# Absolute values of the inspected weights on VectorE instead of ScalarE, and the branch flag made just before the last block of P @ V

## The chip, the cores and the metric

The kernel runs on one core of one Trainium2 chip. The metric is device time of one execution in microseconds, the median of several runs. A separate execution is taken with the hardware profiler; its trace gives the rows shown here, with times counted from the start of its span.

The engines are named as in the profile: PE (TensorE, matmuls; PEld is its weight load), DVE (VectorE), ACT (ScalarE), POOL (GpSimd) and SP (SyncE, which issues most of the DMAs).

## The reference

The kernel computes one transformer layer on x of shape (2, 2048, 256), in float32:

```
xn = layernorm(x)
q, k, v = xn @ Wq, xn @ Wk, xn @ Wv                  # 256 wide, one head
P = softmax(causal(q @ k.T) / 16)
attention = (P @ v) @ Wo
h = silu((xn @ w1.T) * w1_s) * ((xn @ w2.T) * w2_s)  # 1024 wide
h = gelu((h @ h1.T) * h1_s)                          # h1, h2 are 1024 x 1024
h = gelu((h @ h2.T) * h2_s)
out = x + attention + (h @ w3.T) * w3_s
```

w1, w2, h1, h2 and w3 are drawn with entries -1, 0 and 1. The kernel does not rely on it: it looks at the weights as they are and branches.

## The kernel before, in words

**Two stages.** The attention stage runs to about 287 us of the span. Then every engine reads a one-word flag and branches: to the feed-forward part for ternary weights (taken here, `ffn_ternary`, to the end of the span) or to a general one (`ffn`).

**Attention.** The two sequences are cut into eight blocks of 512 rows, n = 0 to 7, four per sequence. Each block has four tiles t of 128 rows. Wk is folded into Wq and Wo into Wv beforehand. For each tile:

- `score` multiplies queries with keys into one of four PSUM banks that are used in turn (`bank()`, ps_0 to ps_3; L401, the causal mask in L407). VectorE copies the bank to SBUF and takes the row maximum on the way (L410). That copy is what frees the bank. After the last bank of a tile comes the negated maximum (L416), the exponential on ScalarE (L422) and, for the wider tiles, a transpose of 32 x 32 blocks on VectorE (L292). Its result is stored to DRAM (d) and fetched back rearranged (e, L304, four DMAs on SP), which completes the transpose of P.
- `turn` makes the two halves of the transposed P: the high half is a cast on ScalarE (L460), the low half a subtraction on GpSimd (L461). Narrow tiles are transposed by TensorE instead (L465), with the halves made by ScalarE (L251) and VectorE (L252).
- `weigh` multiplies both halves with the values, one block of 512 keys at a time (L479 with the high half, L484 with the low half). After the last block of a tile ScalarE scales by the inverse row sum (L499), and GpSimd adds two parts (L500).

Between these the projections of later blocks run: keys (L338, L339), queries (L357) and values (L373). They take their PSUM banks from the same four.

**Looking at the weights.** Beside the attention work, a list `looks` brings weights in by pieces of 128 x 1024 (fetched from the ScalarE queue, L622, into two tags of staging tiles, stg). For the h1 weights VectorE first forms four sums of quarters (L153), which are the factors of a fast matrix product, and SP stores them (L581). Then every piece of h1 and h2 goes through `odd`: take the absolute value in place (L565, ScalarE), then count the elements t for which (t != 0) != t (L567, VectorE), that is, those whose magnitude is neither 0 nor 1. There are sixteen such pieces. Pieces of w1, w2 and w3 go through `low` (L558, a bitwise AND on VectorE; L560, a sum on ScalarE). Each count is one column of `low_bits`.

When all pieces have been looked at, the largest column per partition is taken (L742), a matmul with a column of ones adds it over the partitions (L744), and a cast to an integer makes the flag (L745). In the program this stands at the end of the iteration in which the last look was placed. Each engine loads the flag into a register (L1175) and branches (L1176). Ahead of the branch TensorE has one more piece of work, the last quarter of the first feed-forward block (L172).

**What sets the order.** The program is written as one stream; a layer below reorders each engine's instructions by a model of their times when the program is built, so that moving one instruction can shift others on every engine. `tc.issue_after(mark)` keeps an instruction behind a marked one: marks["DVE"] is the latest score copy (L410), marks["ACT"] the latest exponential, marks["PE"] the latest L484 matmul. On the chip each engine works through its own list in order, a DMA issue included, and waits on semaphores.

Of the kernel before, what the change touches and what calls it, by code (L numbers as in the profile page):

```python
# [9 lines left out]
F32 = mybir.dt.float32  # L10
# [3 lines left out]
U32 = mybir.dt.uint32  # L14
AF = mybir.ActivationFunctionType
ALU = mybir.AluOpType
AX = mybir.AxisListType
# [3 lines left out]
P = 128  # L21
TB = 512
NT = TB // P
# [15 lines left out]
STEPS = [("A11", "B11"), ("S1", "T1"), ("S2", "T2"), ("S4", "B22"), ("S3", "T3"), ("A12", "B21"), ("A22", "T4")]  # L39

SLOTS = {"h1": range(7), "h2": (0, 4, 1, 3, 2, 5, 6)}
LOW_BITS = 0xFFF


# [20 lines left out]
def attn_ffn_kernel(  # L65
# [35 lines left out]
    nc = tc.nc  # L101
# [3 lines left out]
    N = B * NB  # L105
# [14 lines left out]
    flag = const.tile([1, 1], I32, name="flag")  # L120
# [68 lines left out]
    with ExitStack() as actx:  # L189
# [9 lines left out]
        small = actx.enter_context(tc.tile_pool(name="small", bufs=4))  # L199
# [6 lines left out]
        def in_turn(key, tiles):  # L206
            turns[key] += 1
            return tiles[(turns[key] - 1) % len(tiles)]

        def bank():  # L210
            return in_turn("ps", ps_tiles)
# [27 lines left out]
        ones = cp.tile([P, 1], F32, name="ones")  # L239
# [9 lines left out]
        def hi_lo(hi, lo, src):  # L249

            nc.scalar.copy(hi, src)  # L251
            nc.vector.tensor_tensor(lo, src, hi.bitcast(F32), ALU.subtract)  # L252
# [131 lines left out]
        marks = {}  # L384
# [49 lines left out]
        def by_blocks(n, t, m):  # L434
            kt = (n % NB) * NT + t + 1
            u = (m % NB) * NT // UK * UK
            return min(UK, kt - u) >= LEAST and (n, t) != (N - 1, NT - 1)
# [8 lines left out]
        def turn(n, t, m):  # L446
# [20 lines left out]
                )  # L467
            hi_lo(pT[:, 0, :w], pT[:, 1, :w], pt[:, :w])

        def weigh(n, t, m):  # L470
            first = n - n % NB
            st = state[n, t]
            if m == first:
                st["po"] = ps_o.tile([P, 2, D], F32, tag="po", name=f"po_{n}_{t}")
            tiles = NT if m < n else t + 1
            pT = st.pop(m)

            for j in range(tiles):
                nc.tensor.matmul(  # L479
                    out=st["po"], lhsT=pT[:, 0, ts(j, P)], rhs=vs[m][:, j, :, :],  # L480
                    start=(m == first and j == 0), stop=False,
                )
            for j in range(tiles):
                marks["PE"] = nc.tensor.matmul(  # L484
                    out=st["po"][:, 0, :], lhsT=pT[:, 1, ts(j, P)], rhs=vs[m][:, j, 0, :],
                    start=False, stop=(m == n and j == tiles - 1),
                ).ins
            if m == n:
                total = small.tile([P, 1], F32, tag="total", name=f"total_{n}_{t}")
                nc.vector.reduce_sum(total, st["sums"][:, : (n - first) * NT // UK + 1], axis=AX.X)  # L490
                inv = small.tile([P, 1], F32, tag="inv", name=f"inv_{n}_{t}")
                nc.vector.reciprocal(inv, total)
                if n not in attn:
                    attn[n] = rp.tile([P, NT + 1, D], F32, tag="r", name=f"r_{n}"), []
                r, made = attn[n]

                up = n < NB
                two = r[:, ds(t, 2), :]
                nc.scalar.activation(two, st["po"], AF.Copy, scale=inv)  # L499
                nc.gpsimd.tensor_tensor(two[:, int(up), :], two[:, 0, :], two[:, 1, :], ALU.add)  # L500
                made.append(t)
                if len(made) == NT:
                    assert made == sorted(made, reverse=up)
                    nc.sync.dma_start(out=r_d[n], in_=r[:, ds(int(up), NT), :].rearrange("p t d -> p (t d)"))
                del state[n, t]

        def score_steps(n, t):
            order = list(range(n - n % NB, n + 1))
            return [
                (6 * (TB if m < n else (t + 1) * P), lambda m=m: score(n, t, m, order))  # L510
                for m in order
            ]

        def weigh_steps(g, until):

            steps = []
            while g < len(blocks) and blocks[g][0] <= until:
                while turned[0] <= min(g + LEAD, len(blocks) - 1) and (
                    turned[0] <= g or blocks[turned[0]][0] <= until + 1
                ):  # L520
                    b = blocks[turned[0]]
                    steps.append((0 if by_blocks(*b[1:]) else 2 * TB, lambda b=b: turn(*b[1:])))
                    turned[0] += 1
                _, n, t, m = blocks[g]
                steps.append((6 * TB if m < n else 6 * P * (t + 1), lambda b=blocks[g]: weigh(*b[1:])))
                g += 1
            return g, steps
# [13 lines left out]
        low_bits = cp.tile([P, 32], F32, name="low_bits")  # L541
        looked = [0]
        looks = []

        def seen():
            looked[0] += 1
            return low_bits[:, looked[0] - 1 : looked[0]]
# [4 lines left out]
        def low(tiles, dst):  # L552
# [4 lines left out]
            with tc.issue_after(marks["DVE"]):  # L557
                nc.vector.tensor_scalar(tb, tb, LOW_BITS, None, ALU.bitwise_and)  # L558
            with tc.issue_after(marks["ACT"]):
                nc.scalar.activation(t, tb, AF.Copy, accum_out=seen())  # L560

        def odd(t):

            with tc.issue_after(marks["ACT"]):
                nc.scalar.activation(t, t, AF.Abs)  # L565
            with tc.issue_after(marks["DVE"]):
                nc.vector.scalar_tensor_tensor(  # L567
                    t, t, 0.0, t, ALU.not_equal, ALU.not_equal, accum_out=seen()
                )
# [21 lines left out]
        def item_signs(src):  # L591
            items.append(([src], [(0, lambda t: odd(t[0]))]))
# [26 lines left out]
        def fetched_weights(i):  # L619
            for src in items[i][0]:  # L620
                t = stgp.tile([P, SC], F32, tag="stg", name=f"stg_{i}_{len(tiles_of[i])}")
                nc.scalar.dma_start(out=t, in_=src)  # L622
                tiles_of[i].append(t)
# [4 lines left out]
        looks = [(0, lambda: fetched_weights(0))]  # L628
# [73 lines left out]
        def before(j):  # L702
            if 3 <= j < 3 + NB:
                n = NB + j - 3
                x1 = xs[n] = load_x(n)
                with tc.issue_after(marks["DVE"]):
                    stats(x1, mv1[:, j - 3], n)
            if j == 3 + NB:
                with tc.issue_after(marks["ACT"]):
                    r = root(mv1.rearrange("p n t k -> p (n t) k"), NB * NT, "1")  # L710
                for i in range(NB):
                    rstds[NB + i] = [a[:, ts(i, NT)] for a in r]
            if j in TURN_KEYS:
                turn_keys(NB + TURN_KEYS.index(j))
# [2 lines left out]
        now = 0  # L717
        until = -1
        j = -1
        checked = False  # L720
        while until < len(tiles) - 1:
            j += 1
            while until + 1 <= j - AHEAD:
                delay = DELAY_BLOCKS if by_blocks(*tiles[until + 1], 0) else DELAY
                if j <= len(tiles) and now < scored[until + 1] + delay:
                    break
                until += 1
            before(j)
            a = []
            if j < len(tiles):  # L730
                a = score_steps(*tiles[j])
                if j == 0:
                    a = []
            a = a + extra.get(j, [])
            weighed, b = weigh_steps(weighed, until)
            now += sum(cost for cost, _ in a + b)
            scored.append(now)
            merged(a, b, beside)
            if not looks and not checked:
                checked = True  # L740
                most = small.tile([P, 1], F32, tag="most", name="most")
                nc.vector.reduce_max(most, low_bits[:, : looked[0]], axis=AX.X)  # L742
                pf = bank()
                nc.tensor.matmul(out=pf[:1, :1], lhsT=most, rhs=ones, start=True, stop=True)  # L744
                nc.vector.tensor_copy(flag, pf[:1, :1])  # L745

        assert checked
        last_quarter = [bank(), bank()]
        with tc.issue_after(marks["PE"]):
            gated_products(last_quarter, xh0, HK - 1)  # L750
# [1 line left out]
    def ffn_ternary(actx):  # L752
# [208 lines left out]
        def fetch_factors():  # L961
            while factor_order and len(factor_tiles) < 3:
# [3 lines left out]
                    out=w.bitcast(F32).rearrange("p c o -> p (c o)"),  # L966
                    in_=factors[layer][:, SLOTS[layer][step]].rearrange("p c o -> p (c o)"),
                )
# [205 lines left out]

    some = nc.values_load(flag[0:1, 0:1], min_val=0, max_val=LOW_BITS * SC * P)  # L1175
    with tc.If(some == 0) as cmp:  # L1176
# [45 lines left out]
```

## Time and profile before

| | us |
|---|---|
| median of 3 runs (lowest to highest) | 871.73 (871.02 to 874.87) |
| the profiled execution's own time | 872.82 |
| its span | 871.1 |
| PE busy (share of the span) | 852.2 (98%) |
| DVE busy | 620.4 (71%) |
| ACT busy | 504.9 (58%) |
| POOL busy | 296.4 (34%) |
| mean granted TensorE clock | 0.990 |

The shares are averages over both stages. [...] In the rows, "x4" is the number of instructions merged into one row; the bracket at the end of a row gives the idle time of that engine just before it and what ended it.

### The profile page before, as it was taken

The numbers are of one execution on the slowest core, as the hardware profiler recorded it, in microseconds if no ns is written. First come the engines' busy times: TensorE is split into PE (matmuls) and PEld (weight loads), VectorE is DVE, ScalarE is ACT, GpSimd is POOL, SyncE is SP. The second block draws the span as 40 slices with busy tenths as digits, with TensorE's granted clock in tenths as the row PEclk, the third lists the DMA queues.
The fourth block names the chain that finished last, engine by engine and source line by source line (L and its number), as shares of the span: only waits on it lengthen the run. The fifth ranks groups of instructions, "written<-read, shape, count | busy, mean of one in ns | idle before, by whom it ended". The sixth has DMA issues, their size and how long they took to land.

```text
span 871.1 us, 12205 instructions
## 1 busy us (share of the span) xinstructions
PE 852.2 (98%) x4280; PEld 720.1 (83%) x4280; DVE 620.4 (71%) x1065; ACT 504.9 (58%) x881; POOL 296.4 (34%) x242
## 2 busy tenths in 40 slices
PE   8999799999999999999999999999999999999997
PEld 5988688888887878888988888988888898888887
DVE  5687664784764699996596596569468648848764
ACT  2556556764666456677256586536557635657670
POOL 4034857433544476550142050025024003502300
PEclk8999989999999999999999999999999999999999
DMA  9876499766792898854334434432444431144411
GB/s 307 331 250 212 152 348 292 265 214 194 251 343 62 340 400 309 312 192 146 111 109 150 144 144 146 148 121 103 146 145 145 146 136 58 50 144 145 145 49 53
DMA packets 62679, 162.53 MB, mean 187 GB/s; under 512 B 6544, under 2 KB 36368, under 8 KB 53264
## 3 DMA queue, kind: packets, MB, share of 16 engines
q1 hardware_dynamic: 56048, 141.73, 46.6%
q10 hardware_dynamic: 5472, 15.73, 5.3%
q0 software_dynamic: 1088, 4.19, 1.2%
q8 instruction: 36, 0.59, 0.3%
q14 instruction: 35, 0.29, 0.1%
HBM read 120.21 MB, written 47.71 MB: 193 GB/s over the span
## 4 chain that ended last, share of the span: by engine, by line
PE 75%; DMA 9%; DVE 6%; issue 3%; ACT 3%; POOL 2%; SPq 2%; ACTq 0%; POOLq 0%; DVEq 0%
PE ps_own L850 23%; PE ps L850 23%; PE ps L172 5%; PE ps_own L172 5%; PE ps L401 5%; DMA e<-d 4%; PE ps_own L1011 4%; PE ps L1011 4%; POOL pT L461 2%; DMA d<-b 2%; PE ps L373 2%; PE po L479 2%; PE ps L357 2%; SPq L304 1%; DMA d_x<-b 1%
## 5 line engine op out<-in xcount | busy, mean ns | idle before, releaser
L401 PE MATMUL ps<-k,q 128*128 128x512 f32 (+3 forms) x480 | 109.6, 366 | 0.0
L461 POOL TENSOR_TENSOR pT<-e,pT 128x512 fp32r<-128x512 f32 (+3 forms) x60 | 74.8, 1264 | 72.5 <-ACT pT L460 55.6
L401 PEld LDWEIGHTS ps<-k,q 128*128 128x128 f32 x480 | 82.0, 189 | 12.2
L479 PE MATMUL po<-v,pT 128*128 128x512 f32 x272 | 79.6, 406 | 6.6 <-ACT pT L460 6.5
L982 POOL TENSOR_TENSOR rt<-rt,xt 128x1024 f32<-128x1024 f32 x8 | 21.5, 2706 | 165.2 <-issue 114.7
L871 ACT ACTIVATE k_h_u<-k_h_u,h_s_sb 128x512 f32<-128x512 f32 x64 | 45.9, 722 | 38.1 <-DVE k_h_u L870 37.5
L830 POOL TENSOR_TENSOR k_h_u<-k_h_p,k_h_u 128x512 f32<-128x512 f32 x16 | 23.2, 1452 | 123.1 <-ACT q L185 106.3
L479 PEld LDWEIGHTS po<-v,pT 128*128 128x128 f32 x272 | 48.1, 193 | 14.5 <-ACT pT L460 7.2
L410 DVE TENSOR_SCALAR_CACHE_REDUCE s<-ps 128x512 f32<-128x512 f32 (+3 forms) x80 | 47.1, 600 | 12.1 <-PE ps L407 8.1
L422 ACT ACTIVATE s<-s,low 128x1024 f32<-128x1024 f32 (+7 forms) x48 | 43.0, 898 | 21.7 <-DVE low L416 21.7
L292 DVE STREAM_TRANSPOSE b<-s 128x1024 f32<-128x1024 f32 (+3 forms) x30 | 33.5, 1128 | 22.8 <-ACT s L422 20.5
L460 ACT CAST pT<-e 128x512 fp32r<-128x512 f32 (+3 forms) x60 | 32.4, 574 | 27.4 <-DMA e<-d 25.0
L484 PEld LDWEIGHTS po<-v,pT 128*128 128x128 f32 x272 | 42.0, 190 | 6.5 <-POOL pT L461 1.7
L484 PE MATMUL po<-v,pT 128*128 128x256 f32 x272 | 46.9, 286 | 0.2 <-POOL pT L461 0.2
L186 DVE TENSOR_TENSOR q<-k_h_u,q 128x512 fp32r<-128x512 f32 x32 | 45.9, 1462 | 0.0
L889 POOL TENSOR_TENSOR k_h_p<-f_h_B,k_h_p 128x512 f32<-128x512 f32 x16 | 34.4, 2175 | 21.2 <-DVE h_h_T L186 21.2
L500 POOL TENSOR_TENSOR r<-r 128x256 f32<-128x256 f32 x32 | 24.4, 765 | 49.7 <-ACT r L499 49.7
L830 POOL TENSOR_TENSOR f_w_B<-f_w_B,f_w_B 128x512 f32<-128x512 f32 x16 | 26.0, 1646 | 33.0 <-DVE f_w_B L181 33.0
L172 PE MATMUL ps<-xh,w_sb 128*128 128x512 f32 x144 | 35.9, 392 | 0.0
L870 DVE TENSOR_TENSOR k_h_u<-ps_own,k_h_u 128x512 f32<-128x512 f32 x32 | 21.7, 686 | 17.8 <-PE ps_own L850 17.8
L871 ACT ACTIVATE k_h_p<-k_h_p,h_s_sb 128x512 f32<-128x512 f32 x32 | 22.8, 722 | 18.6 <-DVE k_h_p L870 18.6
L850 PE MATMUL ps<-q,w_h_A 128*128 128x512 f32 x128 | 31.2, 393 | 1.5 <-DVE f_w_B L181 1.5
(176 smaller groups left out, 2201.3 us busy)
## 6 DMA issues: line engine op xcount, KB each, us to landing
w_h_S<-factors_h SPq DMA_DIRECT2D x32, 1024.0 KB, 4.7
w_h_A<-factors_h SPq DMA_DIRECT2D x24, 1024.0 KB, 4.7
d<-b SPq DMA_DIRECT2D x18, 512.0 KB, 3.5
e<-d SPq DMA_DIRECT2D x72, 128.0 KB, 3.6
xT_d<-k SPq DMA_DIRECT2D x8, 1024.0 KB, 7.3
stg<-in_ffn_h_w ACTq DMA_DIRECT2D x16, 512.0 KB, 5.6
x<-in_attn_x SPq DMA_DIRECT2D x16, 256.0 KB, 5.9
factors_h<-xh SPq DMA_DIRECT2D x4, 1024.0 KB, 4.8
```

The costliest lines, as they stand in the source:

```text
L172: nc.tensor.matmul(out=p, lhsT=w[:, c, ts(o, P)], rhs=xh[:, c, a, :], start=(c == 0 and a == 0), stop=(c == DC - 1 and a == 1),)
L186: nc.vector.tensor_tensor(r[:, 1, :], f, r[:, 0, :].bitcast(F32), ALU.subtract)
L401: nc.tensor.matmul(out=ps[:, :w], lhsT=qs[n][:, c, a, ts(t, P)], rhs=ks[m][:, c, b, :w], start=(k == 0), stop=(m < n and k == 3 * DC - 1),)
L410: marks["DVE"] = nc.vector.tensor_scalar(st["s"][:, ds(at, w)], ps[:, :w], 1.0, None, ALU.mult, ALU.max, accum_out=st["tops"][:, m - first ...
L422: marks["ACT"] = nc.scalar.activation(st["s"][:, at], st["s"][:, at], AF.Exp, bias=low, accum_out=st["sums"][:, u // UK : u // UK + 1],).ins
L461: nc.gpsimd.tensor_tensor(lo, src, hi.bitcast(F32), ALU.subtract)
L479: nc.tensor.matmul(out=st["po"], lhsT=pT[:, 0, ts(j, P)], rhs=vs[m][:, j, :, :], start=(m == first and j == 0), stop=False,)
L484: marks["PE"] = nc.tensor.matmul(out=st["po"][:, 0, :], lhsT=pT[:, 1, ts(j, P)], rhs=vs[m][:, j, 0, :], start=False, stop=(m == n and j == ...
L830: nc.gpsimd.tensor_tensor(B["B12"][i], B["B22"][i], B["B12"][i], ALU.subtract)
L850: nc.tensor.matmul(out=out[o], lhsT=w[:, c, ts(o, P)], rhs=sets[right][c][:, a, :], start=(start and c == 0 and a == 0), stop=(c == HK - 1 ...
L871: nc.scalar.activation(C[k][o], r[o] if r else banks[o], AF.Gelu, scale=s[:, at : at + 1])
L1011: nc.tensor.matmul(out=ys[t][:, :D], lhsT=h[c][:, a, ts(t, P)], rhs=w3_sb[:, c, :], start=(c == 0 and a == 0), stop=(c == HC - 1 and a == 1),)
```

## The change

`odd` takes the absolute value on VectorE, by clearing the sign bit with a bitwise AND on the same bytes read as unsigned integers, instead of by the Abs function on ScalarE. It stands behind the latest score copy like the count that follows it.

The three steps that make the flag move into a function `judge`, which is called when the program comes to the last block of P @ V (block 7, tile 3, keys 7). Its matmul is kept behind the latest P @ V matmul.

```diff
+MAGNITUDE = 0x7FFFFFFF
 LOW_BITS = 0xFFF
...
+        def judge():
+
+            assert not looks
+            most = small.tile([P, 1], F32, tag="most", name="most")
+            nc.vector.reduce_max(most, low_bits[:, : looked[0]], axis=AX.X)
+            with tc.issue_after(marks["PE"]):
+                pf = bank()
+                nc.tensor.matmul(out=pf[:1, :1], lhsT=most, rhs=ones, start=True, stop=True)
+            nc.vector.tensor_copy(flag, pf[:1, :1])
+
         def weigh(n, t, m):
+            if (n, t, m) == (N - 1, NT - 1, N - 1):
+                judge()
             first = n - n % NB
...
         def odd(t):
 
-            with tc.issue_after(marks["ACT"]):
-                nc.scalar.activation(t, t, AF.Abs)
             with tc.issue_after(marks["DVE"]):
+                nc.vector.tensor_scalar(t.bitcast(U32), t.bitcast(U32), MAGNITUDE, None, ALU.bitwise_and)
                 nc.vector.scalar_tensor_tensor(
                     t, t, 0.0, t, ALU.not_equal, ALU.not_equal, accum_out=seen()
                 )
...
             merged(a, b, beside)
-            if not looks and not checked:
-                checked = True
-                most = small.tile([P, 1], F32, tag="most", name="most")
-                nc.vector.reduce_max(most, low_bits[:, : looked[0]], axis=AX.X)
-                pf = bank()
-                nc.tensor.matmul(out=pf[:1, :1], lhsT=most, rhs=ones, start=True, stop=True)
-                nc.vector.tensor_copy(flag, pf[:1, :1])
-
-        assert checked
+
         last_quarter = [bank(), bank()]
```

More of the change, by code (lines that the diff above doesn't have):

```diff
@@ L719, in attn_ffn_kernel @@
         j = -1
-        checked = False
         while until < len(tiles) - 1:
```

## The prediction

> **What bounds the kernel now.** I read the page's engine totals, then the list of what TensorE waited for, then the timeline round its one long wait, then busy time by stage, then the groups of the lines that the diff touches. TensorE is busy 98% of the span. The change lies in the attention stage, where the weights are looked at (100 to 287 us), so TensorE's waits are asked for in that stretch alone (engine, line, whom it waited for: us, times, longest):
>
> ```profile
> PE po L479 <- ACT pT L460: 6.5, 4, 4.8
> PE ps L357 <- DVE v L252: 0.5, 1, 0.5
> PE ps L357 <- DVE s L410: 0.3, 1, 0.3
> PE po L484 <- POOL pT L461: 0.2, 1, 0.2
> ```
>
> 7.5 us in all, and one wait is 4.8. Nothing that frees ScalarE or VectorE can pay more than these waits and what follows from them. The timeline of the long wait (start, us long, engine, line):
>
> ```profile
> 102.14 4.38 DVE L153 TENSOR_TENSOR xh<-stg,stg 128x512 fp32r<-128x512 f32 x1
> 103.07 0.46 POOL L461 TENSOR_TENSOR pT<-e,pT 128x128 fp32r<-128x128 f32 x1
> 103.49 2.47 POOL L339 TENSOR_TENSOR k<-x,k 128x512 fp32r<-128x512 f32 x2
> 106.55 0.69 DVE L153 TENSOR_TENSOR xh<-xh,stg 128x512 fp32r<-128x512 f32 x1
> ...
> 107.28 1.06 ACT L565 ACTIVATE stg<-stg 128x1024 f32<-128x1024 f32 x1 [3.80 <-DVE xh L153]
> 107.28 0.69 DVE L153 TENSOR_TENSOR xh<-stg,xh 128x512 fp32r<-128x512 f32 x1
> 108.24 0.60 ACT L460 CAST pT<-e 128x512 fp32r<-128x512 f32 x1
> ...
> 108.89 2.08 PE L479 MATMUL po<-v,pT 128*128 128x512 f32 x4 [4.75 <-ACT pT L460]
> ```
>
> Read it backwards. TensorE (108.89) waits for a cast of P on ScalarE (108.24). That cast stood behind an absolute value (107.28), which waited for VectorE's sums of weights (L153). The first sum, 0.69 us when alone, took 4.38: GpSimd ran without a break to 105.96, and the sum ended 0.55 later. The clock answers the gap (stretch, then busy us of PE, PEld, DVE, ACT, POOL, then the granted clock):
>
> ```profile
> 106.53:109.94 3.41, 1.05 (x3) 0.86 (x4) 2.99 (x6) 2.66 (x4) 1.02 (x1) 0.50 0.30 115
> 109.94:113.36 3.42, 3.42 (x11) 2.60 (x10) 3.42 (x8) 1.44 (x3) 3.42 (x3) 0.50 1.02 299
> ```
>
> It is 0.50 until 113.36, so from 108.89 TensorE loses another 2.2 us (4.47 us at half rate).
>
> **The absolute values.** Sixteen leave ScalarE, sixteen ANDs join VectorE; ScalarE's table loads stay. The nearest row to the AND is the other bitwise AND, L558, same shape and type:
>
> ```profile
> L567 DVE SCALAR_TENSOR_TENSOR stg<-stg 128x1024 f32<-128x1024 f32 x16 | 20.9, 1309 | 2.6 <-ACT stg L565 2.5
> L565 ACT ACTIVATE stg<-stg 128x1024 f32<-128x1024 f32 x16 | 16.6, 1048 | 3.8 <-DVE xh L153 3.8
> L558 DVE TENSOR_SCALAR stg<-stg 128x1024 uint32<-128x1024 uint32 x6 | 6.4, 1060 | 4.9 <-DMA stg<-in_ffn_w_w 3.4 <-POOL w_sb L134 1.5
> ```
>
> ScalarE loses 16 x 1.05 = 16.8 us; VectorE gains 16 x 1.06 = 17.0. L558 is 0.69 at its shortest (GpSimd idle) and 1.76 at its longest (GpSimd had just begun L461), so the ends are 11.0 and 28.2 us. From 110 to 270 VectorE is busy about 105 of 160 us, so on average it fits; what counts is where TensorE is within a microsecond of VectorE.
>
> That place is the long wait itself. The cast no longer stands behind an absolute value. Its data (e) landed by 104.06, so TensorE goes on at about 104.8 instead of 108.89; GpSimd makes the low half right behind L339, from 105.96 to about 107.25, and TensorE comes to the query projection L357 at about 108.7. There it stops again: L357 writes PSUM bank ps_1, which VectorE frees with its score copy L410. In the order in which the changed program's instructions stand, that L410 is behind three sums, now **two ANDs**, L567, a transpose and L567.
>
> - Two ANDs start to start: 2 x 0.62 (alone) to 2 x 1.00, less the 0.46 that L567 waited for ScalarE (107.90 to 108.36): +0.8 to +1.5. GpSimd is idle by then, so I take +0.8.
> - The sums: in the old run GpSimd paused at 105.96, and this let the first sum in. Now its next two L461 are ready, 2 x 1.27 = 2.5 us more. VectorE lost at each GpSimd boundary between 102.14 and 105.96, so I take +2.5; the lower end is 0.
> - So L410 ends at 112.40 + 3.3 = 115.7 and L357 starts at 115.8, not 113.45: **+2.35**; ends -0.15 and +3.0.
> - TensorE then idles from 108.7 to 115.8, longer than the gap that halved the clock before. A second half-rate spell costs 0 (if the gap misses it) to 3.4 (all of one 6.83 us spell); the measured one cost 2.2. I take **+2.0**.
>
> Sum here: +4.4 us (-0.15 to +6.4). The rest of the work of this place (L479, L484, both L357) is the same in both orders, only interleaved otherwise.
>
> [...]
>
> **What is given back.** A TensorE that is later meets casts that are ready: two short waits on L460 (0.29 and 0.58 us, at 144 and 157) should go, **-0.9**; ends 0 and -1.7 (all four short waits). The other fourteen ANDs: TensorE waits for nobody between 164 and 273, and VectorE was not the releaser of more than 0.8 us in the stage, so **0**; the cover is VectorE's 55 idle us and the banks that TensorE holds ahead. Without cover it is 14 x 1.06 = 15 us, and below zero nothing, since no wait is left there to remove.
>
> What queues behind the waiting instructions: on ScalarE the next weight fetch (L622) waits for L567 on VectorE, which is now later, and behind it stand casts of P and the scaling L499. On SP, the store of the sums (L581) waits for the last sum, and four fetches of e stand behind it; 2.5 us later they still land near 119, before TensorE asks for them (about 122).
>
> **The flag.** One reduction, a two-pass matmul, one cast and no new instruction: moved only. On TensorE the matmul goes from 271.04 to just before the last block (282.24). It gives up a 0.36 us wait, but TensorE met a 1.11 us wait for a DMA at 274.19 anyway. The cast becomes VectorE's last step before the branch, and the readers wait for it:
>
> ```profile
> L745 DVE CAST flag<-ps x1: 138/138/138, 273.2 to 273.2; 1x1 int32<-1x1 f32 x1
> L1175 SPq TENSOR_LOAD <-flag x1: 468/468/468, 273.4 to 273.4; - x1
> L1175 DVEq TENSOR_LOAD <-flag x1: 544/544/544, 280.8 to 280.8; - x1
> L1175 PEldq TENSOR_LOAD <-flag x1: 487/487/487, 282.0 to 282.0; - x1
> ```
>
> Matmul 0.19, cast 0.14, load 0.49, branch 0.09 and about 0.2 between them: TensorE's sequencer is past the branch at about 283.4, while the last block and the eight matmuls of the last quarter run to 285.6. Cost **0**, with 2.2 us of cover; bare, 1.1 us; at best -0.55. SP holds its last r_d store behind the flag, but that store waits for GpSimd until 285.44. VectorE's next work in the branch came at 285.80, against about 283.4 now.
>
> **Sum.** The profiled execution took 872.82 us, 871.1 of span and 1.7 around it; it is 1.1 above the median of the three runs. 872.8 + 4.4 - 0.9 + 0 = 876.3, so on the median's footing 871.73 + 3.5 = **875.2 us**. About 0.5% (4.4 us) is what a measurement of this kernel can tell from no change: 867.4 to 876.1 counts as the same.
>
> **Rivals.**
> - *The gap closes* (faster). If the sums get in between GpSimd's instructions or the bank is free earlier, TensorE gets the 4.75 us and the 2.2 us at half clock, less about 1.4 for the wait on the low half: -5.5, 866.2 us. For it: ScalarE's queue was the last link. Against: VectorE's chain to L410 ended at 112.40 with no AND in it. It decides if L410 ends before about 108.
> - *VectorE becomes the bound* (slower). It is busy 16.8 of 20 us from 230 to 250; three or more ANDs there, or ScalarE stuck at L622, add some 6 us to the forecast's 3.5: 881 us, more with a further half-clock spell. It decides once TensorE shows waits for L410 or L252 after 164. Against: none over 0.5 us today.
> - *Nothing is left of it*: the first wait moves from L460 to L357, with the same length and one clock spell: 872 us.
> - That the change isn't made can be ruled out: the order has sixteen rows less on ScalarE and sixteen more on VectorE.
>
> **How the numbers follow.** Forecast 0.62 (its ends -0.15 - 1.7 and +6.4 straddle the 4.4 us bound, 0.30 above and 0.32 within). Gap closes 0.15 (0.13 over the bound). VectorE bound 0.15. Nothing left 0.08. Slower 0.45, same 0.42, faster 0.13. The range, 867.5 to 881.5, leaves out most of the fast rival (0.12) and the far end of the slow one (0.08).
>
> **What would show it.** Right: L460 near 104.2; L153's first sum ending near 109; TensorE's longest wait now at L357, released by L410, 5 to 7.5 us long; a half-clock spell after it; L357 starting near 116; no load of the flag on the critical chain. Wrong: L357 before 112 with the clock at 1.00 (first rival), or TensorE waits on VectorE beyond 164 that sum to over 3 us (second). If the sums end near 106.5 as before, the +2.5 is wrong and the total falls to about +1.

## The result, and the profile after

The changed kernel takes 876.78 us (median of 11 runs, 874.52 to 878.79) against 872.3 us for the kernel before (11 runs); the ratio is 1.0057, with a 95% interval of 1.0040 to 1.0074. A second set of runs on another occasion gave 1.0042 (1.0024 to 1.0061). So it is slower by some 4 to 5 us; 875.2 was predicted. The profiled execution took 874.91 us (span 873.1), 1.9 below the median of its kernel, which matters below.

Line numbers from here on are those of the kernel that is shown. In after, the sums are L154 (L153 before), the score copy L411 (L410), the cast and the low half of P L461 and L462 (L460, L461), the query projection L358 (L357), the new AND L578 and the count L579 (L567).

What TensorE waited for from 100 to 295 us in after (line, whom it waited for: us, times, longest):

```profile
PE ps L358 <- DVE s L411: 6.8, 1, 6.8
PE po L497 <- POOL pT L462: 1.3, 3, 0.9
PE po L492 <- ACT pT L461: 1.0, 2, 0.6
PE ps L402 <- DVE v L253: 0.6, 1, 0.6
```

The wait of 4.8 us for ScalarE's cast is gone. In its place stands one of 6.8 us for VectorE's score copy; the rest sums to 2.9 us, about what it was (2.7). The timeline of after around it, with the same columns as for the kernel before:

```profile
102.31 6.28 DVE L154 TENSOR_TENSOR xh<-stg,stg 128x512 fp32r<-128x512 f32 x1 [0.43 <-DMA stg<-in_ffn_h_w]
...
103.06 2.51 POOL L340 TENSOR_TENSOR k<-x,k 128x512 fp32r<-128x512 f32 x2
...
103.93 1.14 ACT L461 CAST pT<-e 128x512 fp32r<-128x512 f32 x2 [0.80 <-DMA e<-d]
...
105.54 2.49 POOL L462 TENSOR_TENSOR pT<-e,pT 128x512 fp32r<-128x512 f32 x2
...
109.95 1.29 DVE L578 TENSOR_SCALAR stg<-stg 128x1024 uint32<-128x1024 uint32 x2
...
112.85 0.58 ACT L252 CAST pT<-pt 128x512 fp32r<-128x512 f32 x1 [7.78 <-DVE stg L579]
...
114.57 0.69 DVE L411 TENSOR_SCALAR_CACHE_REDUCE s<-ps 128x512 f32<-128x512 f32 x1
...
115.33 2.93 PE L358 MATMUL ps<-k,wqk 128*128 128x512 f32 x6 [6.82 <-DVE s L411]
```

Read it from the end. TensorE (115.33) waited for the copy at 114.57, which stood behind the two ANDs (109.95), their counts and a transpose, all behind the first sum. That sum took 6.28 us and ended at 108.59. GpSimd ran without a break from before 100 us to 108.03: the cast on ScalarE now goes at 103.93, so the two low halves (105.54) follow straight behind L340. ScalarE was held too: its cast of a transposed block (112.85) idled 7.78 us, because a weight fetch ahead of it in its queue waits for the count.

Busy time and clock in two stretches of after (stretch, then busy us of PE, PEld, DVE, ACT, POOL, then the granted clock, DMA share and GB/s):

```profile
108.51:113.63 5.12, 0.00 (x0) 0.00 (x0) 5.09 (x10) 0.78 (x2) 0.00 (x0) 1.00 0.52 175
...
115.33:120.45 5.12, 5.12 (x14) 4.25 (x15) 1.14 (x5) 1.53 (x3) 0.84 (x1) 0.50 1.01 356
```

TensorE does nothing for 6.8 us, and when it starts again the clock is at 0.50 until 120.45. From 115.33 that is 5.12 us at half rate, 2.56 us lost. VectorE is busy all through the wait.

The flag, on TensorE:

```profile
284.58 0.19 PE L478 MATMUL ps<-ones,most 128*1 128x1 f32 x2
...
286.20 3.80 PE L173 MATMUL ps<-xh,w_sb 128*128 128x512 f32 x16
```

The matmul of the flag goes ahead of the last block, and the sixteen matmuls of the first-layer products run on from 286.20 without a gap. No wait at the branch.

**A gauge for comparing kernels.** Every version issues the same 4280 matmuls. I take the start of the 500th (97.5 to 99.2 us, ahead of all the trouble), the 700th (near 141 in before, behind the first collision) and the 1700th (near 333, in the second stage) in each trace. The order of matmuls differs a little between versions, so a difference under 1 us means little. Before: 41.94 us from the 500th to the 700th, 192.49 from there to the 1700th. From the 1700th to the end of the span all versions take 537.0 to 538.0 us (before 538.0), so at most 1 us is decided there. Differences to before, from one profiled execution each, beside the median and the ratio of the timed runs:

| kernel | 500th to 700th | 700th to 1700th | median us | ratio (95% interval) |
|---|---|---|---|---|
| after | +4.0 | -1.8 | 876.78 | 1.0057 (1.0040 to 1.0074) |
| after_again | +4.5 | +1.2 | 875.42 | 1.0042 (1.0024 to 1.0061) |
| and_only | +3.9 | +0.1 | 875.50 | 1.0039 (1.0020 to 1.0059) |
| flag_only | -0.1 | -1.5 | 871.06 | 0.9988 (0.9969 to 1.0006) |
| no_and | +2.7 | +1.8 | 876.12 | 1.0044 (1.0029 to 1.0060) |
| late_odd | +2.7 | +0.4 | 878.74 | 1.0071 (1.0046 to 1.0096) |
| no_low | -0.7 | +2.7 | 875.84 | 1.0055 (1.0040 to 1.0069) |
| no_low_and | -0.7 | +2.3 | 872.27 | 1.0016 (0.9999 to 1.0033) |
| gps_sum | +2.2 | -3.2 | 872.08 | 1.0015 (1.0003 to 1.0027) |
| sums_late | -2.9 | -0.2 | 869.59 | 0.9981 (0.9969 to 0.9993) |
| sums_late_abs | -3.0 | +2.3 | 871.75 | 1.0008 (0.9997 to 1.0020) |
| sums_late_flag | -3.0 | +2.8 | 871.12 | 0.9997 (0.9980 to 1.0014) |
| sums_even | -2.3 | +3.4 | 872.91 | 1.0019 (1.0002 to 1.0035) |

### The profile page after: what moved, and what is told of

Its sections match the earlier page's. It is cut to its first block, busy times and chain, and to the rows that moved or that the text cites. A ratio compares the mean times of both kernels' runs of the same rounds, so it can differ in the third digit from the quotient of the medians.

```text
span 873.1 us, 12201 instructions
## 1 busy us (share of the span) xinstructions
PE 852.6 (98%) x4280; PEld 720.6 (83%) x4280; DVE 636.9 (73%) x1081; ACT 489.6 (56%) x865; POOL 300.3 (34%) x242
## 4 chain that ended last, share of the span: by engine, by line
PE 91%; DVE 3%; DMA 3%; POOL 1%; ACT 1%; SPq 1%; issue 0%; ACTq 0%; POOLq 0%
PE ps_own L853 23%; PE ps L853 23%; PE ps L402 9%; PE ps L173 7%; PE ps_own L173 6%; PE po L492 6%; PE ps_own L1014 4%; PE ps L1014 4%; PE po L497 3%; PE ps L358 3%; PE ps L374 2%; DVE xh L154 1%; DMA e<-d 1%; DMA x<-in_attn_x 1%; DMA stg<-in_ffn_h_w 1%; PE pt L466 1%
## 5 line engine op out<-in xcount | busy, mean ns | idle before, releaser
L462 POOL TENSOR_TENSOR pT<-e,pT 128x512 fp32r<-128x512 f32 (+3 forms) x60 | 77.5, 1307 | 74.4 <-ACT pT L461 69.9
L492 PE MATMUL po<-v,pT 128*128 128x512 f32 x272 | 78.8, 402 | 1.1 <-ACT pT L461 1.0
L461 ACT CAST pT<-e 128x512 fp32r<-128x512 f32 (+3 forms) x60 | 32.8, 575 | 45.1 <-DMA e<-d 28.5
L492 PEld LDWEIGHTS po<-v,pT 128*128 128x128 f32 x272 | 48.1, 191 | 9.4 <-ACT pT L461 1.5
L411 DVE TENSOR_SCALAR_CACHE_REDUCE s<-ps 128x512 f32<-128x512 f32 (+3 forms) x80 | 47.0, 600 | 7.1 <-PE ps L402 2.8
L358 PE MATMUL ps<-k,wqk 128*128 128x512 f32 x96 | 28.6, 443 | 7.9 <-DVE s L411 6.8
L512 ACT ACTIVATE r<-po,inv 128x512 f32<-128x512 f32 x32 | 22.0, 686 | 23.4 <-PE po L497 22.5
```

The lines of the kernel that those rows point to most:

```text
L358: nc.tensor.matmul(out=pp, lhsT=wqk[:, c, a, ts(m, P)], rhs=ks[n][:, c, b, :], start=(k == 0), stop=(k == 3 * DC - 1),)
L411: marks["DVE"] = nc.vector.tensor_scalar(st["s"][:, ds(at, w)], ps[:, :w], 1.0, None, ALU.mult, ALU.max, accum_out=st["tops"][:, m - first ...
L462: nc.gpsimd.tensor_tensor(lo, src, hi.bitcast(F32), ALU.subtract)
L492: nc.tensor.matmul(out=st["po"], lhsT=pT[:, 0, ts(j, P)], rhs=vs[m][:, j, :, :], start=(m == first and j == 0), stop=False,)
```

## The experiments

Theory A is that of the prediction: one collision near 105 us, in which VectorE's first sum is held up by GpSimd, and the release of a PSUM bank comes late behind it and the ANDs. The rivals: the flag (B), VectorE's added 17 us spread over the stage (C), and later D (what the ANDs do to the order), E (the sum is long by itself) and F (late DMA data beyond 140 us).

**Which half of the change costs.** and_only is before with this alone:

```diff
-            with tc.issue_after(marks["ACT"]):
-                nc.scalar.activation(t, t, AF.Abs)
             with tc.issue_after(marks["DVE"]):
+                nc.vector.tensor_scalar(t.bitcast(U32), t.bitcast(U32), MAGNITUDE, None, ALU.bitwise_and)
```

> The kernel before with the first half of the change alone: ANDs on VectorE, flag where it was. Theory A (the bank's release is late at one place: behind a first sum that GpSimd's back-to-back work holds up, and two ANDs, and a half-clock spell follows): the long TensorE wait is for score copy L411, 6 to 7 us, the query projection starts near 115.3, half clock after it, time +3 to +6.5 over before, so 875 to 878.5. Rival B (the flag's later place is what costs): within 1 us of before, 872.3. Rival C (17 us more on VectorE, thinly spread): also 875 to 878.5, but with small TensorE waits on VectorE's lines all over the stage that sum to more than 2 us beyond 125 us.

flag_only is after with these lines turned back, so that only judge() and its call are left of the change.

> The kernel after with the absolute value back on ScalarE: only the flag's later place is left of the change. Theory A: the same wait of 4.7 us for ScalarE's cast near 104 to 109 as before, one half-clock spell, no wait at the branch; within 1 us of before, 872.3. Rival B: +3 us or more over before, with TensorE idle near 283 to 287. Rival C expects no change, like A.

Measured: 1.0039 for the ANDs, 0.9988 for the flag. The trace of and_only has the wait of 6.8 us for L411, with L358 at 115.36; flag_only has the old wait of 4.75 us for the cast. The ANDs' half is the whole loss; the flag costs nothing and may give up to 0.3%. B has fallen.

**Is it the ANDs' time?** no_and leaves them out:

```diff
-                nc.vector.tensor_scalar(t.bitcast(U32), t.bitcast(U32), MAGNITUDE, None, ALU.bitwise_and)
                 nc.vector.scalar_tensor_tensor(
-                    t, t, 0.0, t, ALU.not_equal, ALU.not_equal, accum_out=seen()
+                    t, t, 0.0, t, ALU.not_equal, ALU.is_lt, accum_out=seen()
```

> The kernel after without the 16 ANDs; the counting instruction compares by is_lt instead, so that negative entries are no longer judged by their magnitude (left out of the computation; the same branch is taken). Takes 16.5 us off VectorE. Theory A: the ANDs are the small part of the late bank; the first sum still ends near 108.6 (GpSimd), the query projection starts 1.3 us earlier, near 114.0, after a wait of about 5.5 us with a half-clock spell; time 1.3 to 2 us below after, so 874.8 to 875.5, still above before. Rival C (VectorE's load): back to before or below it, 871 to 872.5. Rival D (the sum is not held up by GpSimd but by what the ANDs do to the order): first sum ends near 106.5, query projection near 112, 871 to 873.

late_odd keeps them and moves them behind the copies:

```diff
-                (1500, lambda t: odd(t[0])),
+                (24000 if c == 0 else 1500, lambda t: odd(t[0])),
```

> The kernel after with one number changed: the looks at the first tile of each factor item of h1 wait for 24000 instead of 1500 units of TensorE work in the first of these items, which puts both ANDs and both counts behind the score copies of tile (1, 2); all the work is still done. Theory A: behind the sums only a transpose stands before the copy L411, which ends near 111.5 instead of 115.2; the query projection starts near 111.6, the wait falls from 6.8 to about 3.3 us; -3.5 us, and up to 2.5 more if the half-clock spell stays away: 870.5 to 873.5. Rival C (load): no change from after, 876.8, as VectorE's work is the same. Rival D (order of ANDs and sums): first sum earlier than 107.

Measured: 1.0044 and 1.0071, no better than after; no_and lies 0.6 us above its range, and late_odd (six runs) 5 us above. The first sum and the query projection in the timeline of no_and:

```profile
99.75 6.88 DVE L154 TENSOR_TENSOR xh<-stg,stg 128x512 fp32r<-128x512 f32 x1
...
112.42 2.93 PE L358 MATMUL ps<-k,wqk 128*128 128x512 f32 x6 [7.64 <-DVE s L411]
```

And the same two in that of late_odd:

```profile
100.77 7.94 DVE L154 TENSOR_TENSOR xh<-stg,stg 128x512 fp32r<-128x512 f32 x1
...
112.19 5.02 PE L358 MATMUL ps<-k,wqk 128*128 128x512 f32 x12 [7.10 <-DVE s L411]
```

In both the projection does start 3 us earlier than in after, yet the wait is 7.1 to 7.6 us: TensorE's order had changed as well, and it now came to L358 near 105 us, with matmuls left for later that after had done before. The sum is what stays. It started earlier and only took longer, 6.88 and 7.94 us, because it ends when GpSimd does (106.09 and 108.16). So the start of one instruction is a poor measure once the order changes; with the gauge, the ANDs at this place are worth 1.3 us (4.0 to 2.7), as expected, and the sum is the larger part. That taking off all sixteen ANDs (VectorE's busy time fell from 636.9 to 627.0 us, not by the 16.5 expected) changed the ratio only from 1.0057 to 1.0044 speaks against C. In no_and the sum ends at 106.63 and the projection starts at 112.42, both as D said; but the sum had begun at 99.75, 2.6 us earlier than in after, and still ended only with GpSimd's run. With a sum that ends at 108.71 in late_odd, where D wanted less than 107, D has fallen.

**Is it GpSimd that holds the sum?** no_low leaves out the two low halves of P that ran beside it:

```diff
-                nc.gpsimd.tensor_tensor(lo, src, hi.bitcast(F32), ALU.subtract)
+                if (n, t) != (2, 3) or m > 1:
+                    nc.gpsimd.tensor_tensor(lo, src, hi.bitcast(F32), ALU.subtract)
```

(and the matmuls of these two blocks take the high halves twice).

> The kernel after without GpSimd's two low halves of P for tile (2, 3), blocks 0 and 1 (left out of the computation: the matmuls that would read them read the high halves once more, so TensorE's work is the same). These are the two L462 that ran at 105.5 to 108.0 while the first sum stood. Theory A (GpSimd's unbroken run holds VectorE's first sum): GpSimd falls idle near 105.6, the first sum ends near 106.2 instead of 108.6, the query projection starts near 113.0 instead of 115.3; 2 to 3 us below after, 874 to 875. Theory E (the first sum is long for a reason of its own): it still ends near 108.5 and the time is that of after, 876.5. Theory C (17 us more on VectorE over the whole stage): also no change.

gps_sum instead gives the first sum to GpSimd:

```diff
-            steps = [(0, lambda t: sum_up(t, 0))]
+            steps = [(0, lambda t: sum_up(t, 0, nc.gpsimd if c == 0 else nc.vector))]
```

> The kernel after with the first of the four sums, in the first factor item alone, made by GpSimd instead of VectorE; in the order that follows, one more sum and then the score copy L411 stand ahead of the ANDs. Theory A: GpSimd takes about 1.3 us for it (its L462 of this shape takes 1.27); the sum behind it is the one that GpSimd's L340 and L462 now hold up, to about 109, then L411, and the query projection starts near 110 instead of 115.3; 4 to 6 us below after, 870.5 to 873. Theory E (the sum is long by itself): the same, as the sum is off VectorE, but no long operation on VectorE. Theory C: 876.5, no change.

The sum, GpSimd's last piece and TensorE's new wait in the timeline of no_low (its L493 is L492 of after):

```profile
99.86 4.80 DVE L154 TENSOR_TENSOR xh<-stg,stg 128x512 fp32r<-128x512 f32 x1
...
101.56 2.55 POOL L340 TENSOR_TENSOR k<-x,k 128x512 fp32r<-128x512 f32 x2
...
109.56 2.07 PE L493 MATMUL po<-v,pT 128*128 128x512 f32 x4 [3.54 <-ACT pT L252]
```

The sum on GpSimd and the next sum on VectorE in that of gps_sum:

```profile
102.76 1.30 POOL L154 TENSOR_TENSOR xh<-stg,stg 128x512 fp32r<-128x512 f32 x1
...
105.33 6.07 DVE L154 TENSOR_TENSOR xh<-xh,stg 128x512 fp32r<-128x512 f32 x1
```

E has fallen. In no_low the sum ends at 104.66, 0.55 us behind GpSimd's 104.11, and L358 starts at 111.43; no_low reached its 500th matmul 1.4 us earlier than after, so this is 112.8 on after's footing (113.0 expected). In gps_sum GpSimd takes 1.30 us for the sum, and the *next* two-input sum of VectorE, 0.69 us when alone, stands 6.07 us, to 0.54 us behind GpSimd's last piece (110.86). At this place it holds in all fourteen profiles: the sum ends 0.54 to 0.56 us after GpSimd's unbroken run, and takes 3.46 to 7.94 us according to when it started. It is not so everywhere. Later in the same traces sums of the same kind get in between two of GpSimd's instructions, as in after:

```profile
145.29 2.80 POOL L462 TENSOR_TENSOR pT<-e,pT 128x512 fp32r<-128x512 f32 x2 [0.30 <-ACT pT L461]
...
145.58 1.65 DVE L154 TENSOR_TENSOR xh<-xh,stg 128x512 fp32r<-128x512 f32 x1
```

The first of these two L462 ends at 146.68, the second starts at once, and the sum still ends at 147.23, 0.55 us behind the first; the second takes 1.45 us instead of 1.27. So what no_low and gps_sum show is that GpSimd's run holds the sum at this place; why VectorE is passed over there at every boundary, and not later, stays open.

gps_sum came out at 872.08, inside its range, in part by luck: L358 started at 112.07 after a wait of 6.71 us, 2 us later than expected, and 3.2 us of its time against before came back behind the 700th matmul, which Theory A does not explain. The time of no_low did not follow its place (875.84, above its 874 to 875): what it won by the 700th matmul (4.7 us against after) it had lost by the 1700th.

**Take the sums out of the way.** sums_late is after with the first factor item begun later (its gap was 15000):

```diff
-            looks.append((gap, lambda i=i, f=steps[0][1]: f(tiles_of[i])))
+            looks.append((45000 if i == 4 else gap, lambda i=i, f=steps[0][1]: f(tiles_of[i])))
```

> The kernel after with one number changed: the first factor item of h1 begins 45000 units of TensorE work after the look ahead of it instead of 8000 or more, so that its sums, ANDs and counts stand behind the score copies L411 of tile (1, 2). All the work is still done. Theory A: nothing slow stands ahead of L411, the bank is free before TensorE asks, near 108; the wait of 6.8 us for L411 shrinks below 1.5 us, TensorE's idle time from 100 to 125 us falls from 8.1 to about 2, no half-clock spell there (2.6 us); 7 to 9 us below after, 867.5 to 870, which is below before too. Theory C: 876 or more, with waits for VectorE's lines spread over the stage. Theory E: like A here.

sums_late_abs is before, with the same edit.

> The kernel before with the same number changed, so the absolute value still on ScalarE. Theory A (the place is what costs, not the engine of the absolute value): the wait of 4.7 us for ScalarE's cast goes as well, with its half-clock spell (2.2 us): 4 to 6 us below before, 866 to 868, and within 1.5 us of the other kernel with late sums. Theory C (17 us more on VectorE cost in themselves): 3 us or more faster than the other kernel with late sums. Theory E: like A.

The timeline of sums_late:

```profile
104.00 1.25 DVE L293 STREAM_TRANSPOSE b<-s 128x1024 f32<-128x1024 f32 x1 [1.75 <-DMA d<-b]
...
105.38 0.69 DVE L411 TENSOR_SCALAR_CACHE_REDUCE s<-ps 128x512 f32<-128x512 f32 x1
...
105.99 3.46 DVE L154 TENSOR_TENSOR xh<-stg,stg 128x512 fp32r<-128x512 f32 x1
...
106.13 1.66 PE L358 MATMUL ps<-k,wqk 128*128 128x512 f32 x6 [1.28 <-DVE s L411]
...
109.98 1.43 PE L358 MATMUL ps<-k,wqk 128*128 128x512 f32 x5 [2.19 <-DVE s L411]
```

While GpSimd works from 99.62 to 108.91, a transpose (one input) takes its usual 1.25 us and the score copy out of PSUM its usual 0.69; only the two-input sum is held, 3.46 us. The first copy now goes ahead of it, and the one wait of 6.8 us becomes 1.28 and 2.19 (one below 1.5 was expected), since the layer that orders the instructions put a sum between the two copies. The clock stays at 1.00 through it. At 869.59 us this is the only version whose interval lies below before, and so the one that beats both kernels: 0.9981 (0.9969 to 0.9993), a gain of about 0.2% over before and 7.2 us below after, inside its range; measured against before it is less than the half per cent that was set as the bound. The result for sums_late_abs, 871.75, missed its 866 to 868. Up to the 1400th matmul (near 263 us) the two kernels run alike, 164.85 and 164.64 us from the 500th. Then TensorE in sums_late_abs waits for the reduction ahead of the early flag (line numbers of before):

```profile
271.05 0.19 PE L744 MATMUL ps<-ones,most 128*1 128x1 f32 x2 [2.07 <-DVE most L742]
```

So I held the 2.2 us between them to be the flag's place, and tried that with the absolute value on ScalarE, the late flag and the late sums (sums_late_flag, the edit of sums_late in flag_only):

> The kernel of late sums with the absolute value back on ScalarE, but the flag at its later place. Theory A (which engine makes the absolute value does not matter once the sums are out of the way; the difference of 2.2 us between the two kernels with late sums was TensorE's wait of 2.1 us for the reduction ahead of the early flag): within 1.2 us of the kernel with late sums, 869.6, and no wait for the reduction. Theory C (17 us more on VectorE cost in themselves): 2 us or more faster than that, 867.5 or less.

TensorE's wait near that place in the timeline of sums_late_flag:

```profile
271.44 1.43 PE L492 MATMUL po<-v,pT 128*128 128x512 f32 x4 [2.54 <-ACT pT L461]
```

Measured: 871.12, no wait for the reduction, but one of 2.54 us at the same place, for a cast on ScalarE, and a half-clock spell of 3.41 us behind it, as in sums_late_abs. The flag's wait had only covered another one, so that reading has fallen. Whether the 1.5 us that sums_late has over it belong to the AND stays open: the intervals of the two ratios overlap, and ScalarE at 267.3 us waited for a weight whose fetch went out at 264.11, in sums_late at 259.81, and the trace does not tell how much of that is the AND's. C, which wanted the AND to be 2 us slower here, is refuted.

**Can the rest be had?** sums_even multiplies all later gaps of sums_late by 0.886, so that the looks end where they used to:

```diff
+            looks = [(g if k < 18 else g * 0.886, f) for k, (g, f) in enumerate(looks)]
```

> The kernel of late sums (ANDs on VectorE, late flag) with all later gaps between looks multiplied by 0.886, so that the looks end about where they ended in after, and not 30000 units later. Theory A: the waits of 1.4 us for the load of xh and of 1.0 for a cast near 256 to 267 go; 867 to 869.5. Rival: a denser sequence of looks collides elsewhere, with new waits for VectorE in the stage: 870.5 or more.

Measured: 872.91. The rival was right: TensorE now idles 3.05 us from 150 to 200 us (0.81 in sums_late), in five waits of 0.25 to 1.47 us for VectorE and for casts.

**Where did no_low's gain go?** no_low_and has the edits of no_low and of no_and together.

> The kernel after without the two low halves of P of tile (2, 3) and without the ANDs (both left out as before). Theory F (what was won at 115 us is given back between 140 and 165 us to data that DMAs bring late, so VectorE's load is not it): TensorE still idles 2 us or more from 140 to 165 us, and the time is 874 to 876, at most 1.5 below the kernel without low halves alone (875.8). Theory C: the waits from 140 to 165 us go, 871.5 to 873.

Measured: 872.27, 3.6 us below no_low, which is C's time; but TensorE still idles 3.1 us from 125 to 200 us, with one wait of 2.85 at 145 for a cast whose data a DMA brought, which is what F expected. The two profiled executions differ by 0.4 us only (236.41 and 236.05 from the 500th to the 1700th), but that of no_low is the fastest of its six runs, 2.8 us below their median. I can't settle it: with this collision gone, some of the ANDs between 140 and 250 us may well cost something, though gps_sum and sums_late carry all sixteen and lose nothing there.

**The shown profile is a lucky one.** after_again is after, unchanged, profiled once more.

> The kernel after, unchanged, profiled once more: its first profiled execution (874.9) lies 1.9 us below the median of its runs (876.8), so its trace accounts for 2.1 of the 5 us only. Theory A: the cluster at 100 to 125 us costs the same as in the first profile (query projection near 115.3 less the offset of the start, wait of 6.8 us, half clock behind it), 4 us over before; what differs between executions is what comes back from 140 to 290 us, 1.8 us in the first profile, 0 to 1 in a slower execution. Rival: the cluster itself is longer in a typical execution, with a wait of 8 us or more.

Measured: an execution of 878.87 us, the slowest of eight (median 875.42). The sum takes 7.28 us, the wait is 6.82 again, L358 starts at 116.14, and 4.5 us are lost by the 700th matmul (4.0 in the first profile). The first execution then regained 1.8 us up to the 1700th; this one lost a further 1.2, where 0 to 1 us back was expected. The cluster costs the same in both; what comes back behind it does not.

## Why the prediction was right, point by point

- *The wait moves from the cast to the bank.* Right: the cast at 103.93 (104.2 said), TensorE on at 104.60 (104.8), at L358 by 108.51 (108.7), which then waits for L411 6.82 us (5 to 7.5).
- *Sums, +2.5.* The first sum ended at 108.59 where 109 was said: +2.07 against 106.52. The mechanism was inferred from one row; no_low and gps_sum now show it for this place. That VectorE would go on losing was a lucky guess all the same: in the same trace of before the sum at 185.13 got in at the first boundary (it ended at 186.22, 0.55 us behind the L461 that ended at 185.67, and the next L461 had followed at once). The rest of the error is that GpSimd's L340 began 0.43 us earlier than the L339 of before, so its run was through at 108.03.
- *Two ANDs, +0.8.* The pair took 1.21 us start to start at this place, as reckoned (1.24 less 0.46). All sixteen: median 0.687 us, longest 1.82; VectorE's busy time rose by 16.5 us (17.0 said).
- *L357 +2.35.* L358 at 115.33 against 113.45, +1.9; L411 ended at 115.26 instead of 115.7.
- *Half clock, +2.0.* One spell of 6.83 us as before, from 113.63, of which TensorE lost 2.56 us. Sum of the place: 4.4 predicted; +4.0 and +4.5 by the gauge in two profiles. That the sum fits so well is partly luck: the start of L357 was put 0.5 us too late and the half clock 0.6 us too low, and the two cancel.
- *Given back, -0.9.* This is the mis-sized term: -1.8 in one execution, +1.2 in the other. Of the two waits that should go, that at 144 went in both; that at 157 stayed, 0.64 and 0.69 us at the same matmul (159.86 and 160.94). What else made up the 1.8 us is not shown: flag_only, which has no collision to make good beyond that of before, gains 1.5 over the same stretch, and and_only +0.1. A single figure was not to be had from one trace, and the timed loss of 4 to 5 us (3.5 predicted) suggests that on average nothing came back.
- *The other fourteen ANDs, 0.* Held in after: no wait for VectorE above 0.6 us beyond 125 us. no_low against no_low_and leaves a doubt that it would hold for a TensorE that is earlier.
- *The flag, 0.* Right: flag_only 0.9988 (0.9969 to 1.0006). The waits of 0.36 and 1.11 us quoted there are those of the weight loads; TensorE's matmul waited 0.91 us at 274.19, and less than 0.2 at 271.04.
- *GpSimd beside the ANDs.* The forecast has no term for it. GpSimd's busy time rose by 3.9 us (300.3 against 296.4); the two low halves beside the held sum took 2.49 us, no more than a pair without one (2.53 at 119.61). There the waiting was VectorE's; beside later ANDs GpSimd waited too (the L462 from 161.01 to 162.77, 1.76 us instead of 1.27, beside the ANDs at 160.20 and 161.60).
- *Rivals.* The closing gap came true only once the sums were moved; in after, VectorE was not the bound beyond the one place.

## What to carry to other kernels

A wait that ends on one engine can hide a second one right behind it: work out, for the instruction that follows on the waiting engine, who releases that and what the change puts ahead of it. Before moving work between engines, look where it lands among the neighbours' unbroken runs; in after, moving the place of the first item's sums (one number) won 7.2 us, where moving the engine had lost 4; in before the same move of the place won nothing that the timed runs show (1.0008). And take more than one profile before a term of a microsecond is booked as given back.

## What the runs showed of the hardware that was not expected

- Near 105 us a sum on VectorE with two SBUF inputs waited for as long as GpSimd ran back to back, and not for one instruction: it took 3.46 to 7.94 us for 0.69 us of work, ending 0.54 to 0.56 us after GpSimd's last one, in fourteen of fourteen profiles, and was passed over at two (sums_late) to seven (late_odd) boundaries between GpSimd's instructions. Later, from 110 to 300 us, four sums in the traces of before (141.51 and 185.13) and after (145.58 and 189.31) got in between two GpSimd instructions at the first boundary, ending 0.55 to 0.63 us behind the first of the two, and so did five counts, 1.08 to 1.13 us behind it (before at 110.68, 194.22 and 244.40; after at 247.59 and 263.55). What makes the difference stays open. Beside GpSimd's run near 105 us in sums_late a one-input transpose (104.00, 1.25 us) and a read of PSUM (105.38, 0.69) were not slowed.
- The half-clock spells came in two lengths, 6.83 us (before, 106.53 to 113.36; after, 113.62 to 120.45) and 3.41 us. TensorE waits of 4.75 to 7.6 us were followed by the long one, waits of 3.5 to 3.9 (no_low, no_low_and) by the short one, and waits of 2.1 to 2.9 by the short one (no_low_and at 145, sums_late_abs and sums_late_flag at 272) or by none (2.10 in no_and at 208, and 2.19 to 2.50 in the four kernels with late sums at 110). Each spell by the first collision cost TensorE 1.7 to 2.7 us; of the long ones a part passed while TensorE still waited. TensorE had not been wholly idle ahead of each: from 142.01 to 145.42 in no_low_and it was busy 0.56 us, and the four matmuls from 145.04 took 1.76 us (L493; four at 105.07 took 1.09); from 269.53 to 272.94 in sums_late_abs it was busy 1.43 us, and the four from 272.90 took 1.22 (L484; four at 265.77 took 0.64).
